# An attention product in which one of sixteen squares is cut in two

## The chip, the cores and the metric

The kernel runs on one core of one Trainium2 chip. The metric is the device time of one execution in microseconds (us); lower is better. A run is executed several times, and the median is compared. TensorE multiplies (the profile calls its matmuls PE and the loading of their weights PEld), VectorE is DVE, ScalarE is ACT, GpSimd is POOL, and SyncE (SP) issues transfers.

## The reference

The reference is a cross-attention with two contexts, all in float32. There are 2 batches of 2048 tokens with 640 channels, in 20 heads of 32 channels. The context has 154 tokens per batch with 1024 channels: 77 of text and 77 of image, each with its own weights for keys and values. Softmax is taken over the 77 text tokens and the 77 image tokens apart, and the two results are added.

```python
residual = hidden_states                       # (2, 2048, 640)
text = encoder_hidden_states[:, :77, :]
ip = encoder_hidden_states[:, 77:, :]
q = _split_heads(hidden_states @ Wq.T, H)      # 20 heads of 32
k = _split_heads(text @ Wk.T, H)
v = _split_heads(text @ Wv.T, H)
out_text = _merge_heads(_attend(q, k, v, sm_scale))
k_ip = _split_heads(ip @ Wk_ip.T, H)
v_ip = _split_heads(ip @ Wv_ip.T, H)
out_ip = _merge_heads(_attend(q, k_ip, v_ip, sm_scale))
out = out_text + IP_SCALE * out_ip             # IP_SCALE = 1
out = out @ Wo.T + bo
return out + residual
```

`_attend` is softmax(q k^T / sqrt(32)) v.

## The kernel before, in words

Channels lie on the 128 partitions, so that 640 channels are 5 chunks of 128, and a chunk is 4 heads of 32. A batch and a chunk together are one attention product `q`, from 0 to 9 (`NP` = 10). The 2048 tokens of a batch are two halves of 1024, so that a unit `u` is half of a `q` and there are 20 units. In the text below, the attention products are numbered in words, from the first to the tenth.

For each unit the queries are projected (`queries`, line 194) and scaled by ScalarE (line 204), and then scores are made in three groups of token tiles (`scores`, line 226). ScalarE copies the scores into the tile `pb` (line 238). VectorE takes the maximum of each row (line 251), POOL subtracts it (line 265), ScalarE takes the exponential (line 272), VectorE sums (line 297) and inverts (line 304), POOL multiplies (line 309), and VectorE transposes every 32x32 block of `pb` in place (line 316). The 154 keys of a token are padded to 160, that is five blocks of 32 (`NK` = 5).

`attend` (line 325) then multiplies the probabilities of a whole `q` by the values. TensorE's array of 128x128 is used as sixteen squares of 32x32. Row group `r` (32 partitions of the input) holds one of four groups of tokens, and column group `g` (32 partitions of the output) is a head. In each of the five rounds `k`, one for each block of keys, there are 16 matmuls, one for each square, in the order r = 0..3 and within it g = 0..3. Each takes 32x32 weights from `v4s` and 512 columns from `pb`, and adds into PSUM bank `pa[r]` at the partitions of `g`. Square n of a round is r = n // 4, g = n % 4; so square 0 is r = 0, g = 0, and square 1 is r = 0, g = 1. The sixteen squares hold different weights and work side by side, and the five rounds of one square add into the same place. ScalarE then copies the four banks into the tile `aT` (`take_attention`, lines 348 and 352).

The rest is the projections of keys and values (line 133), and the output projection: products of fewer multiplications than the plain form for batch 0 (`product`, lines 483 and 493; last chunk in line 464) and for batch 1 (`F` words, line 841), with sums taken by VectorE and POOL.

The order of all work is written out by hand: `SCHEDULE` is a list of words, and `emit` runs each in turn, so that every engine gets its instructions in the order of the words. `A.q@h` is the attention product q into half h of the eight PSUM banks; `CA.q` is the copy behind it. Semaphores between the engines follow from the data; instructions of one engine need none among themselves. The values' squares `v4s` are loaded by DMA from SP (`spread_v`) ahead of each product.

Of the kernel before, what the change touches and what calls it, by code (L numbers as in the profile page):

```python
# [15 lines left out]
H, D, TEXT = 20, 32, 77  # L16
# [4 lines left out]
def kernel(  # L21
# [25 lines left out]
    nc = tc.nc  # L47
# [3 lines left out]
    G = P // D  # L51
# [3 lines left out]
    NT = BLK // P  # L55
    SUB = S // BLK
# [4 lines left out]
    NK = (2 * L + D - 1) // D  # L61
# [3 lines left out]
    NU = NP * SUB  # L65
    OPEN = 4
    HT = TB // 2

    const = ctx.enter_context(tc.tile_pool(name="const", bufs=1))
    qpool = ctx.enter_context(tc.tile_pool(name="qpool", bufs=5))  # L70
# [11 lines left out]
    v4s = [const.tile([P, G, NK, D], F32, name=f"v4_{n}") for n in range(2)]  # L82
# [235 lines left out]
    def attend(q, pa):  # L318

        zones = pb[:, ds(q % 2, SUB)].rearrange("p z n g (k s) -> p (z n) g k s", k=NK)  # L320
        for k in range(NK):
            for r in range(G):
                rows = slice(r * D, (r + 1) * D)
                for g in range(G):
                    nc.tensor.matmul(  # L325
                        pa[r][g * D : (g + 1) * D, :],
                        v4s[q % 2][rows, g, k, :],
                        zones[rows, :, g, k, :],
                        start=(k == 0),
                        stop=(k == NK - 1),  # L330
                    )

    def rows_of_attention(b, c):


        if b == 0:
            return aT[:, ts(c + 1, NHB)]
        if c == 0:
            return aT[:, ts(0, NHB)]
        return aT[:, NHB + c - 1 : NHB + NHB * NHB : NHB]  # L340
# [55 lines left out]
    def block(b, i, r, h):  # L396
# [3 lines left out]
        )  # L400
        return aT[:, m : n + 1 : n - m, ts(h, HT)]

# [38 lines left out]
    def in_dram(t, b, i, s, h):  # L441
        return t[: (NC - 1) * P].rearrange("(op s p) t -> s p op t", s=2, p=P)[
            s, :, :, ds(b * S + i * TB + h * HT, HT)
        ]
# [31 lines left out]
    def product(m, b, i, ps):  # L476
# [3 lines left out]
        for op in range(2):  # L480
            part = ps[:, ts(op, HT)]
            for kp in range(2):
# [8 lines left out]
            if fifth:  # L491
# [3 lines left out]
                    w_last[:, op] if s is None else wo[:, NC - 1, ts(2 * op + s, P)],  # L495
                    rows_of_attention(b, NC - 1)[:, i, ts(h, HT)],
                    start=False,
# [4 lines left out]
    def take_product(m, b, i, ps):  # L502
        part = {2: (0, 0), 1: (0, 0), 5: (1, 1), 7: (1, 1), 3: (0, 1), 6: (0, 1), 4: (1, 0)}[m]
        t = part_in(sums_of(b, i), *part)
        if m in (5, 3, 4, 1 if b else 2):
            for op in range(2):
                bias = bo_sb[:, ds(2 * op + part[0], 1)]
                nc.vector.scalar_tensor_tensor(
                    t[:, op], ps[:, ts(op, HT)], bias, t[:, op], ALU.add, ALU.add
                )  # L510
# [117 lines left out]
    def emit(word):  # L628
# [7 lines left out]
        elif k == "A":  # L636
            at[name] = halves[int(where)]
            attend(x, at[name])
        elif k == "CA":
            take_attention(x, at[f"A.{x}"])  # L640
# [243 lines left out]
```

## Time and profile before

| what | us |
|---|---|
| median of three runs | 500.54 |
| lowest and highest of the three | 499.85, 500.70 |
| the profiled execution | 499.79 |
| its span, first to last instruction | 498.0 |

| engine | busy us | instructions |
|---|---|---|
| TensorE matmul (PE) | 491.1 | 4114 |
| TensorE weight load (PEld) | 291.1 | 4114 |
| VectorE (DVE) | 425.7 | 388 |
| POOL | 425.7 | 189 |
| ScalarE (ACT) | 243.0 | 423 |

| matmuls of | records | busy us |
|---|---|---|
| queries, line 194 | 400 | 178.2 |
| scores, line 226 | 1280 | 57.0 |
| attention products, line 325 | 1600 | 55.7 |
| keys and values, line 133 | 320 | 45.9 |

How to read it: times count from the first instruction. Matmuls overlap in the array, and the end of each is modelled, so that their busy time is no sum of work; the start of each is what the text goes by. In a row of the timeline, instructions of one line are merged: the first number is the start, the second the length until the last of them ends, and x is the count. A row for a narrow window holds the instructions that run in that window, from the start of the first of them. In a row of windows, the stretch is followed by its length and the busy time, with the count of instructions that run in it; then come the granted clock of TensorE, the busy share of the DMA engines and GB/s. The granted clock was full (1.00) throughout. The chain of waits is followed back from the last instruction, and gives the share of the span in which each engine or line held the end.

### The profile page before, as it was taken

The numbers are of one execution on the slowest core, as the hardware profiler recorded it, in microseconds if no ns is written. First come the engines' busy times: TensorE is split into PE (matmuls) and PEld (weight loads), VectorE is DVE, ScalarE is ACT, GpSimd is POOL, SyncE is SP. The second block draws the span as 40 slices with busy tenths as digits, with TensorE's granted clock in tenths as the row PEclk, the third lists the DMA queues.
The fourth block names the chain that finished last, engine by engine and source line by source line (L and its number), as shares of the span: only waits on it lengthen the run. The fifth ranks groups of instructions, "written<-read, shape, count | busy, mean of one in ns | idle before, by whom it ended". The sixth has DMA issues, their size and how long they took to land.

```text
span 498.0 us, 9768 instructions
## 1 busy us (share of the span) xinstructions
PE 491.1 (99%) x4114; PEld 291.1 (58%) x4114; DVE 425.7 (85%) x388; ACT 243.0 (49%) x423; POOL 425.7 (85%) x189
## 2 busy tenths in 40 slices
PE   9999999999999999999999999999999999999997
PEld 4667658558658555457655655744665575444442
DVE  0078998999989899969996888899699999998985
ACT  1276747667757567566616554647473543100000
POOL 0089799999999999998998999899999999397790
PEclk9999999999999999999999999999999999999999
DMA  8985300354253665794074367554524101510026
GB/s 262 355 238 151 108 15 1 86 110 118 57 161 122 177 214 165 247 333 150 1 253 154 123 200 256 151 165 161 200 64 133 45 2 64 169 64 22 0 105 232
DMA packets 66987, 70.15 MB, mean 141 GB/s; under 512 B 3712, under 2 KB 46720, under 8 KB 66944
## 3 DMA queue, kind: packets, MB, share of 16 engines
q1 hardware_dynamic: 66224, 68.81, 44.4%
q8 instruction: 32, 0.52, 0.4%
q10 hardware_dynamic: 720, 0.72, 0.4%
q14 instruction: 11, 0.09, 0.1%
HBM read 58.21 MB, written 11.30 MB: 140 GB/s over the span
## 4 chain that ended last, share of the span: by engine, by line
PE 66%; POOL 15%; DVE 11%; DMA 3%; ACT 2%; issue 2%; SPq 1%; POOLq 0%
PE bank L194 23%; PE bank L841 11%; POOL pb L265 8%; PE bank L325 8%; PE bank L226 8%; PE bank L133 6%; POOL pb L309 6%; PE bank L483 5%; DVE pb L316 4%; PE bank L464 3%; DVE den L297 3%; DVE mx L251 2%; DMA aT<-in_L_xattn_Wk_ip_dram 2%; DMA wq<-in_L_xattn_Wq_dram 2%; PE bank L493 1%
## 5 line engine op out<-in xcount | busy, mean ns | idle before, releaser
L265 POOL TENSOR_TENSOR pb<-pb,mx 128x1848 f32<-128x1848 f32 (+1 forms) x60 | 175.6, 2944 | 32.1 <-DVE mx L251 31.5
L309 POOL TENSOR_TENSOR pb<-pb,rden 128x1848 f32<-128x1848 f32 (+1 forms) x60 | 175.7, 2945 | 13.2 <-DVE rden L304 12.6
L194 PE MATMUL bank<-x,wq 128*128 128x512 f32 x400 | 178.2, 597 | 0.2
L251 DVE TENSOR_REDUCE mx<-pb 128x24 f32<-128x1848 f32 (+1 forms) x60 | 109.8, 1839 | 30.0 <-ACT pb L238 29.6
L272 ACT ACTIVATE pb<-pb 128x1848 f32<-128x1848 f32 (+1 forms) x60 | 94.3, 1578 | 65.6 <-POOL pb L265 65.5
L194 PEld LDWEIGHTS bank<-x,wq 128*128 128x128 f32 x400 | 74.0, 190 | 88.9 <-issue 81.4
L316 DVE STREAM_TRANSPOSE pb<-pb 128x1920 f32<-128x1920 f32 (+1 forms) x60 | 115.4, 1933 | 7.0 <-POOL pb L309 7.0
L297 DVE TENSOR_REDUCE den<-pb 128x24 f32<-128x1848 f32 (+1 forms) x60 | 110.0, 1840 | 11.6 <-ACT pb L272 11.3
L238 ACT COPY pb<-bank 128x462 f32<-128x462 f32 (+1 forms) x240 | 101.9, 536 | 36.7 <-PE bank L226 36.0
L226 PEld LDWEIGHTS bank<-kT,qT 32*128 32x128 f32 x1280 | 46.5, 184 | 23.8 <-issue 16.4
L226 PE MATMUL bank<-kT,qT 32*128 32x154 f32 x1280 | 57.0, 305 | 0.3 <-ACT kT L550 0.3
L325 PE MATMUL bank<-pb,v 32*32 32x512 f32 x1600 | 55.7, 597 | 0.4 <-DVE pb L316 0.3
L133 PE MATMUL bank<-wo_ct,aT 128*128 128x154 f32 x320 | 45.9, 297 | 0.9 <-ACT aT L352 0.4
L204 ACT ACTIVATE qT<-bank 128x512 f32<-128x512 f32 x40 | 23.6, 596 | 46.5 <-PE bank L194 46.5
L133 PEld LDWEIGHTS bank<-wo_ct,aT 128*128 128x128 f32 x320 | 42.9, 188 | 4.4 <-issue 2.4
L325 PEld LDWEIGHTS bank<-pb,v 32*32 32x32 f32 x1600 | 32.1, 103 | 20.8 <-issue 9.5
L464 PE MATMUL bank<-aT,wo_ct 128*128 128x512 f32 x80 | 36.1, 596 | 0.0
L483 PE MATMUL bank<-aT,wo_ct 128*128 128x256 f32 x128 | 32.6, 387 | 0.1
L483 PEld LDWEIGHTS bank<-aT,wo_ct 128*128 128x128 f32 x128 | 23.5, 190 | 7.3 <-issue 3.6
L789 DVE TENSOR_TENSOR x<-x,bank 128x512 f32<-128x512 f32 x36 | 23.1, 681 | 3.4 <-PE bank L841 3.1
L464 PEld LDWEIGHTS bank<-aT,wo_ct 128*128 128x128 f32 x80 | 15.0, 190 | 16.9 <-issue 16.6
L841 PE MATMUL bank<-pb 128*128 128x512 f32 x48 | 22.1, 594 | 0.0
(71 smaller groups left out, 335.1 us busy)
## 6 DMA issues: line engine op xcount, KB each, us to landing
x<-in_x_dram SPq DMA_DIRECT2D x20, 1280.0 KB, 6.8
out_dram<-acc SPq DMA_DIRECT2D x20, 256.0 KB, 2.4
x<-in_x_dram SPq DMA_DIRECT2D x18, 256.0 KB, 5.4
acc<-in_x_dram SPq DMA_DIRECT2D x16, 256.0 KB, 4.1
out_dram<-x SPq DMA_DIRECT2D x15, 256.0 KB, 2.1
v<-scr SPq DMA_DIRECT2D x40, 80.0 KB, 3.3
wq<-in_L_xattn_Wq_dram SPq DMA_DIRECT2D x9, 320.0 KB, 4.9
aT<-in_L_xattn_Wk_dram SPq DMA_DIRECT2D x5, 512.0 KB, 5.4
```

The costliest lines, as they stand in the source:

```text
L133: nc.tensor.matmul(keys_in(out), loaded[n][:, k, :], cT[:, k, :, t, :], start=(k == 0), stop=(k == NCC - 1))
L194: nc.tensor.matmul(pq, wqs[q % 3][:, k, :], xs[place_of(u, h)][:, k, :], start=(k == 0), stop=(k == NC - 1),)
L226: nc.tensor.matmul(ps[g][:, ts(t, 2 * L)], qTs[(u, h)][g * D : (g + 1) * D, ts(st, P)], kT[g * D : (g + 1) * D, c, b].rearrange("p t l -> ...
L238: nc.scalar.copy(keys_of(u, s)[:, :, g], ps[g][:, : n * 2 * L].rearrange("p (n l) -> p n l", n=n))
L251: nc.vector.tensor_reduce(mx, rows_of(u, s), AX.X, ALU.max, negate=by_rows(u, s))
L265: nc.gpsimd.tensor_tensor(rows_of(u, s), rows_of(u, s), maxs[(u, s)].unsqueeze(3).to_broadcast([P, n, 2, L]), ALU.subtract)
L272: nc.scalar.activation(e, e, AF.Exp)
L297: nc.vector.tensor_reduce(dens[(u, s)], rows_of(u, s), AX.X, ALU.add)
L309: nc.gpsimd.tensor_tensor(rows_of(u, s), rows_of(u, s), rdens[(u, s)].unsqueeze(3).to_broadcast([P, n, 2, L]), ALU.mult)
L316: nc.vector.transpose(p, p)
L325: nc.tensor.matmul(pa[r][g * D : (g + 1) * D, :], v4s[q % 2][rows, g, k, :], zones[rows, :, g, k, :], start=(k == 0), stop=(k == NK - 1),)
L483: nc.tensor.matmul(part, w_of[m][:, kp, op], t_of(m, b, i)[:, kp], start=(op == kp == 0 and m in (1, 2, 5)), stop=(op == 1 and kp == 1 and ...
```

## The change

In the first four rounds of each attention product, square 1 is multiplied in two matmuls with the same weights: token tiles 0 to 12 of its 16 (13 x 32 = 416 columns) in its old place, and tiles 13 to 15 (96 columns) behind square 15 of the same round. The fifth round is as before. In the first round the long part opens its place in PSUM (`start`), and the short part adds to it.

```diff
+    LEAD, LONG = 1, 13
...
+        whole, long, short = slice(0, SUB * NT), slice(0, LONG), slice(LONG, SUB * NT)
         for k in range(NK):
-            for r in range(G):
+            steps = [(n, long if n == LEAD and k < NK - 1 else whole) for n in range(G * G)]
+            if k < NK - 1:
+                steps.append((LEAD, short))
+            for n, part in steps:
+                r, g = divmod(n, G)
                 rows = slice(r * D, (r + 1) * D)
-                for g in range(G):
-                    nc.tensor.matmul(
-                        pa[r][g * D : (g + 1) * D, :],
-                        v4s[q % 2][rows, g, k, :],
-                        zones[rows, :, g, k, :],
-                        start=(k == 0),
-                        stop=(k == NK - 1),
-                    )
+                nc.tensor.matmul(
+                    pa[r][g * D : (g + 1) * D, part.start * D : part.stop * D],
+                    v4s[q % 2][rows, g, k, :],
+                    zones[rows, part, g, k, :],
+                    start=(k == 0 and part is not short),
+                    stop=(k == NK - 1),
+                    skip_group_check=(n == LEAD),
+                )
```

## The prediction

> **What bounds the kernel now.** I read the page first, then the records of line 325, then the loads of single products in order of time, then the chain of waits.
>
> ```profile
> span 498.0 us, 9768 instructions
> PE 491.1 (99%) x4114; PEld 291.1 (58%) x4114; DVE 425.7 (85%) x388; ACT 243.0 (49%) x423; POOL 425.7 (85%) x189
> PE 66%; POOL 15%; DVE 11%; DMA 3%; ACT 2%; issue 2%; SPq 1%; POOLq 0%
> PE bank L194 23%; PE bank L841 11%; POOL pb L265 8%; PE bank L325 8%; PE bank L226 8%; PE bank L133 6%; POOL pb L309 6%; PE bank L483 5%; DVE pb L316 4%; PE bank L464 3%; DVE den L297 3%; DVE mx L251 2%; DMA aT<-in_L_xattn_Wk_ip_dram 2%; DMA wq<-in_L_xattn_Wq_dram 2%; PE bank L493 1%
> L464 PE MATMUL bank<-aT,wo_ct 128*128 128x512 f32 x80 | 36.1, 596 | 0.0
> L483 PE MATMUL bank<-aT,wo_ct 128*128 128x256 f32 x128 | 32.6, 387 | 0.1
> L325 PEld LDWEIGHTS bank<-pb,v x1600: 101/103/106, 69.2 to 432.5; 32*32 32x32 f32 x178
> L325 PE MATMUL bank<-pb,v x1600: 584/588/612, 69.2 to 432.9; 32*32 32x512 f32 x178
> ```
>
> TensorE is busy nearly throughout and holds 66% of the chain, but the chain goes through POOL and VectorE for 26%, and there a longer product costs nothing. Line 325 has 8%. Ten attention products of 5 rounds of 16 squares are 800 products; 1600 loads and 1600 matmuls mean that each product is two passes, each a load and a matmul. A round is thus 16 x 4 = 64 TensorE instructions.
>
> Next, the ten products whole: length, and records in each.
>
> ```profile
> 69.20 5.64 PE L325 MATMUL bank<-pb,v 32*32 32x512 f32 x160
> 106.52 5.52 PE L325 MATMUL bank<-pb,v 32*32 32x512 f32 x160
> 143.67 5.64 PE L325 MATMUL bank<-pb,v 32*32 32x512 f32 x160
> 180.92 5.51 PE L325 MATMUL bank<-pb,v 32*32 32x512 f32 x160
> 212.11 5.51 PE L325 MATMUL bank<-pb,v 32*32 32x512 f32 x160
> 261.28 5.57 PE L325 MATMUL bank<-pb,v 32*32 32x512 f32 x160
> 303.71 5.67 PE L325 MATMUL bank<-pb,v 32*32 32x512 f32 x160
> 346.85 5.53 PE L325 MATMUL bank<-pb,v 32*32 32x512 f32 x160
> 392.07 5.55 PE L325 MATMUL bank<-pb,v 32*32 32x512 f32 x160
> 427.96 5.52 PE L325 MATMUL bank<-pb,v 32*32 32x512 f32 x160 [0.25 <-DVE pb L316]
> ```
>
> Inside the fourth (from 180.92), the weight loads in order of time; the last two of these rows are from narrower windows of the same view. Then two instants of the seventh.
>
> ```profile
> 180.89 0.27 PEld L325 LDWEIGHTS bank<-pb,v 32*32 32x32 f32 x32 [0.16 <-issue]
> 181.35 0.10 PEld L325 LDWEIGHTS bank<-pb,v 32*32 32x32 f32 x1 [0.19 <-issue]
> 181.78 0.57 PEld L325 LDWEIGHTS bank<-pb,v 32*32 32x32 f32 x32 [0.33 <-issue]
> 181.97 0.10 PEld L325 LDWEIGHTS bank<-pb,v 32*32 32x32 f32 x1
> 185.19 0.33 PEld L325 LDWEIGHTS bank<-pb,v 32*32 32x32 f32 x24
> ...
> 181.35 1.35 PE L325 MATMUL bank<-pb,v 32*32 32x512 f32 x24
> ...
> 304.30 1.14 PE L325 MATMUL bank<-pb,v 32*32 32x512 f32 x17
> 304.92 0.18 PEld L325 LDWEIGHTS bank<-pb,v 32*32 32x32 f32 x7
> ```
>
> All 32 loads of round 1 go within 0.27 us. At 181.35 square 0 starts its second pass, 0.43 after its first (180.92), and the 33rd load (square 0, round 2) goes at once; the 34th waits for the matmul that it follows (181.78, another 0.43). Then the 35th, square 1's, waits until 181.97. That is 0.62 after square 0's second pass of round 1 began (181.35): its 0.588 record and 0.03. In the seventh product the second pass of square 4 began at 304.30 (the first still running at 304.80, squares 0 to 3 being out by then) and the round-2 load of square 5 went at 304.92, again 0.62 later. So I read: TensorE holds 64 instructions, one round, in order; a place is free only when the instruction 64 before has ended, with all ahead of it. A square of round k+1 may load 0.62 after the square **before** it began its second pass of round k. From a square's first load to its second pass is 0.46 (180.89 to 181.35), so a round takes 0.62 + 0.46 = 1.08, where two passes of 0.43 are 0.86. In each round the wave's end comes forward by one square's place, as each square follows its left neighbour. The 24 loads of 12 squares from 185.19 take 0.33 - 0.10 = 0.23, about 18 ns a square.
>
> **The change part by part.** Nothing moves on a DMA queue, SP, POOL, VectorE or ScalarE. Per product 4 squares become two: 4 x 2 more loads and as many matmuls, 160 of each in all; no columns are added.
>
> *The two sizes.* No row has 96 or 416 columns. From the L464 and L483 rows, (596 - 387) / 256 = 0.82 ns a column: estimates of 0.08 and 0.34 us of streaming, as ends 0.02 and 0.43 (another slope; a whole pass). In round 1, counted from its start, square 1's long passes run 0.03 to 0.37 and 0.37 to 0.72, and the first short pass 0.72 to 0.80. This fits, as the other squares run until about 1.0.
>
> *The places in the queue.* Instructions 65 to 68 are now the short piece, not square 0 of round 2. The 67th entry is free at once; the 68th, the short second pass, needs instruction 4, square 0's second pass, out: 0.43 + 0.62 = 1.05. So the short piece ends at about 1.15 and square 0 of round 2 loads at 1.05, not 0.43. It loses its lead, which nobody used: before, square 1 waited until 181.97 - 180.92 = 1.05 anyway. Square 1 starts at 1.15, late by 0.1; it is one of 16 starting over 1.05 to 1.31, so I cost it at zero; without the cover of the other squares it costs 0.1 us.
>
> *The lockstep.* With 68 instructions a round, a square hangs on **its own** second pass of the round before, no longer on its left neighbour's. The period stays 1.08, but the wave no longer gains a place each round. From round 2 to round 5 that loses 3 places of 18 ns, 54, and I take 0.06 us per product. Ends: 0, if the neighbour rule is kept after all, and 0.05 + 0.10 = 0.15, if square 1's late start of 0.1 is not covered in the end.
>
> *Products that stagger in round 1.* In some, semaphore waits split round 1 by groups of four squares.
>
> ```profile
> L325 PEldq EVENT_SEMAPHORE  x2: 51/51/51, 261.3 to 261.5; - x2
> 303.70:303.75 0.05, 0.04 (x4) 1.00 1.05 410
> 303.87:303.90 0.03, 0.03 (x8) 1.00 0.88 341
> 304.01:304.04 0.03, 0.03 (x12) 1.00 1.57 614
> 304.14:304.15 0.01, 0.01 (x14) 1.00 1.57 614
> ```
>
> In the seventh product 4, 8, 12 and then more matmuls are under way at 303.70, .87, 304.01, .14: steps of about 0.14. The first, second, third, sixth and seventh product have such a wait ahead of the last four squares (the sixth's two waits, the later at 261.5, are shown). Now the last square of round 5 hangs, three places back, on a square ahead of that gap; after the change on itself, behind it. I take 0.12 us for each, as the gap is partly worked off by the 18 ns pitch; ends 0.06 (the gap is worked off wholly) and 0.06 + 0.14 = 0.20.
>
> *What reaches the end.* The chain in order of time: its pieces around the products that it leaves out, and one product that it goes through.
>
> ```profile
> 137.47 8.28 POOL pb L265 x3
> ...
> 179.04 3.29 POOL pb L265
> ...
> 212.11 5.51 PE bank L325 x153
> ...
> 391.78 2.22 POOL pb L265
> ```
>
> It passes by the products at 143.67, 180.92 and 392.07, where POOL and VectorE hold it: 0.12 + 0.06 + 0.06 is hidden, and counts if that cover is gone. The other seven it goes through as it does at 212.11: three unstaggered (212.11, 346.85, 427.96) and four staggered ones, 3 x 0.06 + 4 x 0.12 = **0.66 us**. All ten would give 5 x 0.06 + 5 x 0.12 = 0.90. The ends: 0 and 5 x 0.15 + 5 x 0.20 = 1.75. The profiled execution took 499.79, 0.75 below the median of the three runs (500.54); 499.79 + 0.66 = 500.45, and from the median **501.2**.
>
> *A rule of the skill against the change.* At 181.35 a load goes into rows on which squares 0 to 3 are still multiplying (second passes of 0.588 from 181.35 on). The Trainium skill, "TensorE: Matmul & The Clock Gate", Part 3, "What overlaps and what doesn't", says that a weight load overlaps matmuls under way only where their row group is another one. By that rule the short piece would be far dearer (last rival below); the trace does not agree, since the load of 181.35 did not wait. The same page gives the queue as 64 deep with a partial reorder window; by that figure the sum stays 0.66, and the first and second rivals below lose, since both need a wait that is no queue.
>
> **The rivals.**
> 1. *Faster.* The wait of 0.19 (181.78 to 181.97) is no queue: it falls only on a tile that goes on without a break, as square 0 does. The short piece then breaks square 0's run. Square 2 of round 2 would load at 0.94 instead of 1.08 (0.72 + 0.19 for the second short load, then two loads), and later rounds would take 0.34 + 0.34 + 0.03 + 0.19 + 0.02 = 0.92 instead of 1.08: 0.14 + 3 x 0.16 = 0.62, less 0.05 for the lost lead, 0.57 on seven products: 4.0 us, 496.5. Against it: only square 0 got its load of round 2 ahead (the 33rd) and ran on; square 4 in the row of 304.30 did not, and still square 5 waited 0.62 for it.
> 2. *No change.* Each square's own results must drain, and the queue is wide enough. Then the neighbour rule stays as it was, and the extra pieces cost two loads: about 0.02 per product, 0.1 in all: 500.6. The rows of before cannot tell this from the queue, since a round is just 64 instructions; but 32 loads and one more and then nothing is what 64 places look like.
> 3. *Slower.* A short piece holds its four places as long as a whole square, 1.08. Then a round costs 68/64 of 1.08, 0.067 more; over four rounds 0.27, on seven products 1.9, on ten 2.7: 502.4 to 503.2. It decides once the piece's places are wanted before it has ended. By my working it ends about 0.4 us before the last square of the next round needs them, which is a thin margin with the short second pass entering so late.
> 4. *Slower by far.* Loads wait for the whole row group: each short pass then waits until squares 2 and 3 are out (1.06), and costs its own 0.08, a drain of 0.16 (0.588 - 0.43) and 0.03, twice; the next round starts at 1.62 instead of 1.05. 0.57 x 4 rounds x 7 to 10 products: 517 to 523.
>
> **How the numbers follow.** A change of 0.2%, 1.0 us, is about what a measurement of this kernel tells from none, as its three runs spread over 0.85. The lost lead: 0.50, its own range 500.5 to 502.3 (0 to 1.75 on the median), of which 0.32 within 0.2% and 0.18 slower. Rival 1, with partial gains of the same kind: 0.19, faster. Rival 2: 0.10, same. Rival 3: 0.19, slower. Rival 4: 0.02, slower. Faster 0.19, same 0.42, slower 0.39. The range 498.2 to 503.2 takes in part of rival 1's gain and all of rival 3; outside are rival 4, the full gain of rival 1 and a loss above 2.7.
>
> **What would show it.** Right: 1680 records of loads and matmuls on the product's line, 176 in each product; lengths of about 5.57 for the unstaggered ones (the ones at 181 and 212) and 5.64 to 5.80 for the staggered; in the first round no load of square 0 at +0.43, but one of the short piece at about +0.38 and square 0's at +1.05; round after round 1.08 apart. Rival 1 shows as rounds of 0.92 and products of about 5.0; rival 3 as rounds of 1.14; rival 4 as products near 7.8. The ends on the chain: the product at 212 should pass its 0.06 on, the one at 181 should not. My forecast is wrong if the products get shorter at all, if the short piece's second pass starts well before +1.05 (then places are not freed in order), or if the chain goes through other products afterwards.

## The result, and the profile after

The changed kernel takes 504.16 us (median of five executions, 502.86 to 505.40) where the kernel before takes 500.54 (499.85 to 500.70). The ratio is 1.008, with a 95% interval of 1.0057 to 1.0103: slower by 0.8%, and above the predicted range of 498.2 to 503.2. The profiled execution of the changed kernel took 502.86, and its span is 501.1; the kernel before had 499.79 and 498.0. The traces explain these 3.07 us. The median lies 1.3 above the profiled execution, and the times scatter three times as widely as before; only the profiled execution has a trace, so that the cause of the scatter can only be inferred.

First the page of the changed kernel: span, busy time, chain by engine, the two groups of the product's line (330 now), and the queue that brings instructions.

```profile
span 501.1 us, 9928 instructions
PE 493.7 (99%) x4194; PEld 289.2 (58%) x4194; DVE 425.9 (85%) x388; ACT 242.9 (48%) x423; POOL 425.6 (85%) x189
PE 80%; POOL 8%; DVE 8%; issue 2%; ACT 1%; POOLq 0%
L330 PE MATMUL bank<-pb,v 32*32 32x512 f32 (+2 forms) x1680 | 58.1, 577 | 1.1 <-issue 0.9
L330 PEld LDWEIGHTS bank<-pb,v 32*32 32x32 f32 x1680 | 29.4, 103 | 26.6 <-issue 23.2
q8 instruction: 33, 0.54, 0.4%
```

And the rows of the page before that answer to the last three.

```profile
L325 PE MATMUL bank<-pb,v 32*32 32x512 f32 x1600 | 55.7, 597 | 0.4 <-DVE pb L316 0.3
L325 PEld LDWEIGHTS bank<-pb,v 32*32 32x32 f32 x1600 | 32.1, 103 | 20.8 <-issue 9.5
q8 instruction: 32, 0.52, 0.4%
```

There are 80 matmuls and 80 loads more, as in the prediction's 1680 records of each. (Its "160 of each in all" is a slip: 160 is the number of both together.) New are 0.9 us of idle time ahead of matmuls that no engine ended ("issue"), and one more packet on the queue for instructions: 33 packets, 0.54 MB, so 16 KB each.

The ten products of the changed kernel, as the prediction showed them: start, length to the last end, records (168 matmuls each).

```profile
68.92 5.80 PE L330 MATMUL bank<-pb,v 32*32 32x512 f32 x168
106.38 5.64 PE L330 MATMUL bank<-pb,v 32*32 32x512 f32 x168
143.69 5.93 PE L330 MATMUL bank<-pb,v 32*32 32x512 f32 x168
181.21 5.89 PE L330 MATMUL bank<-pb,v 32*32 32x512 f32 x168
212.72 5.52 PE L330 MATMUL bank<-pb,v 32*32 32x512 f32 x162
219.13 1.05 PE L330 MATMUL bank<-pb,v 32*32 32x512 f32 x6 [0.89 <-issue]
263.85 5.68 PE L330 MATMUL bank<-pb,v 32*32 32x512 f32 x168
306.40 5.79 PE L330 MATMUL bank<-pb,v 32*32 32x512 f32 x168
349.67 5.59 PE L330 MATMUL bank<-pb,v 32*32 32x512 f32 x168
394.95 5.61 PE L330 MATMUL bank<-pb,v 32*32 32x512 f32 x168
430.81 5.59 PE L330 MATMUL bank<-pb,v 32*32 32x512 f32 x168
```

The fifth product stands in two rows: after 162 of its 168 matmuls nothing starts until 219.13, and it lasts 7.46 us (212.72 to 220.18) instead of 5.51. Set against the rows of before, product by product, from the records' own nanoseconds:

| product | 1st | 2nd | 3rd | 4th | 5th | 6th | 7th | 8th | 9th | 10th | sum |
|---|---|---|---|---|---|---|---|---|---|---|---|
| longer by, us | 0.16 | 0.12 | 0.29 | 0.37 | 1.95 | 0.11 | 0.12 | 0.06 | 0.07 | 0.06 | 3.32 |
| forecast, us | 0.12 | 0.12 | 0.12 | 0.06 | 0.06 | 0.12 | 0.12 | 0.06 | 0.06 | 0.06 | 0.90 |

The eleven stretches between and around the products give -0.26 together, -0.28 of it ahead of the first product. 3.32 - 0.26 is the 3.07 of the profiled executions. So the whole loss lies in the products, and nearly all of it reaches the end. Seven of them are as forecast within 0.04; the third, fourth and fifth are 0.17, 0.31 and 1.89 above, 2.37 in sum.

Round 1 of the fourth product looks as the prediction drew it. Its weight loads in order of time:

```profile
181.21 0.23 PEld L330 LDWEIGHTS bank<-pb,v 32*32 32x32 f32 x32 [0.16 <-issue]
181.59 0.10 PEld L330 LDWEIGHTS bank<-pb,v 32*32 32x32 f32 x1 [0.15 <-issue]
181.94 0.10 PEld L330 LDWEIGHTS bank<-pb,v 32*32 32x32 f32 x1 [0.24 <-issue]
182.28 0.53 PEld L330 LDWEIGHTS bank<-pb,v 32*32 32x32 f32 x33 [0.24 <-issue]
```

The short piece loads 0.38 after the start and again 0.73 after it; square 0 of round 2 comes at 1.07, no longer at 0.43. The short piece's second matmul starts at 1.07 too, where the prediction had 1.05. What goes wrong in the fifth product is of another kind. The end of it, from the timeline of all engines in a narrow window:

```profile
216.43 1.81 PE L330 MATMUL bank<-pb,v 32*32 32x512 f32 x40
216.99 0.34 PEld L330 LDWEIGHTS bank<-pb,v 32*32 32x32 f32 x26 [0.19 <-issue]
...
219.13 0.15 PEld L330 LDWEIGHTS bank<-pb,v 32*32 32x32 f32 x6 [1.80 <-issue]
219.13 1.05 PE L330 MATMUL bank<-pb,v 32*32 32x512 f32 x6 [0.89 <-issue]
```

The last start ahead of the gap is at 217.65, the next at 219.13, and by 218.24 the array has run empty. No semaphore and no engine ends that wait. The queue of 64 does not either, since its places are all free by then. The stretches around it, with the DMA engines' share and rate as the last two columns:

```profile
212.50:215.50 3.00, 2.98 (x104) 1.58 (x101) 3.00 (x3) 1.89 (x4) 2.56 (x3) 1.00 1.09 356
215.50:217.70 2.20, 2.20 (x91) 1.04 (x61) 2.20 (x2) 0.00 (x0) 2.20 (x1) 1.00 1.15 238
217.70:219.10 1.40, 0.54 (x20) 0.00 (x0) 0.20 (x1) 0.95 (x2) 1.40 (x2) 1.00 1.05 319
```

The share of the DMA engines (the time of all packets, so that it can pass 1) stays above 1.0 through all three stretches. And in the transfers between 216.3 and 217.8 there is one packet for instructions, which by its record moved from 216.34 to 217.72:

```profile
q1 hardware_dynamic: 355, 0.32, 108.8%
q8 instruction: 1, 0.02, 5.8%
```

This gave the theory for the experiments, called the supply theory below: TensorE's instructions come in blocks of 16 KB over the same DMA engines as the data. An attention product uses them up fast, 64 in 1.07 us for five rounds on end, while a projection of queries takes 0.43 us for a load and a matmul; a group of scores is nearly as dense, but is over after 24 to 40 matmuls and their loads. Where a limit between two blocks falls into a product and the next block is late, TensorE stands still. The change adds 160 instructions, and so moves every later limit to another place in the work.

### The profile page after: what moved, and what is told of

It reads as the page before. It is cut to its first block, busy times and chain, and to the rows that moved or that the text cites. A ratio compares the mean times of both kernels' runs of the same rounds, so it can differ in the third digit from the quotient of the medians.

```text
span 501.1 us, 9928 instructions
## 1 busy us (share of the span) xinstructions
PE 493.7 (99%) x4194; PEld 289.2 (58%) x4194; DVE 425.9 (85%) x388; ACT 242.9 (48%) x423; POOL 425.6 (85%) x189
## 4 chain that ended last, share of the span: by engine, by line
PE 80%; POOL 8%; DVE 8%; issue 2%; ACT 1%; POOLq 0%
PE bank L195 31%; PE bank L847 11%; PE bank L330 10%; PE bank L227 9%; PE bank L134 9%; PE bank L489 5%; POOL pb L310 4%; POOL pb L266 4%; PE bank L470 3%; DVE pb L317 3%; DVE den L298 2%; DVE mx L252 1%; PE bank L499 1%; POOL aT L430 1%; PE bank L546 1%
## 5 line engine op out<-in xcount | busy, mean ns | idle before, releaser
L330 PE MATMUL bank<-pb,v 32*32 32x512 f32 (+2 forms) x1680 | 58.1, 577 | 1.1 <-issue 0.9
L330 PEld LDWEIGHTS bank<-pb,v 32*32 32x32 f32 x1680 | 29.4, 103 | 26.6 <-issue 23.2
L358 ACT COPY aT<-bank 128x256 f32<-128x256 f32 x40 | 11.5, 413 | 23.3 <-PE bank L330 23.3
```

Of the source, the lines that this page charges most:

```text
L330: nc.tensor.matmul(pa[r][g * D : (g + 1) * D, part.start * D : part.stop * D], v4s[q % 2][rows, g, k, :], zones[rows, part, g, k, :], star ...
```

## The experiments

Times and ratios are against the kernel before on the same chip (medians of 499.99 to 500.12); the ratios are those on record, which differ from the quotient of the medians by up to 0.2%. "Longer by" is the sum over the ten products in the profiled execution, against the profile of before.

**e1: the change, its instructions moved by 132.** Seven warm-up matmuls ahead of all work become forty small ones, so that each product starts 132 entries later in TensorE's order (a matmul here is two passes with a load each).

```diff
-    for _ in range(7):
-        nc.tensor.matmul(banks[0][:, :P], warm, warm, start=True, stop=True)
+    for _ in range(40):
+        nc.tensor.matmul(banks[0][:D, :D], warm[:, :D], warm[:, :D], start=True, stop=True)
```

> The cut as in the change; the 7 warm-up matmuls (128 columns) are replaced by 40 small ones (32 columns), so that TensorE's later instructions stand 132 places further on. Theory (instruction supply): TensorE's instructions come 256 at a time, and a product stalls when two limits between such blocks fall into it. With 132 places only the ninth product has two. So the stalls in the third, fourth and fifth product (0.17, 0.31 and 1.89 us) go, every product has the length of the lost lead alone (5.57 to 5.80 us), and the time is 500.9 to 501.6. Rival (the cut itself holds the queue): the fifth product stays near 7.5 us and the time near 503 to 504.

Measured: 502.29 us, ratio 1.004 (1.0028 to 1.0052). The third, fourth and fifth product:

```profile
144.98 5.75 PE L330 MATMUL bank<-pb,v 32*32 32x512 f32 x168
182.32 5.58 PE L330 MATMUL bank<-pb,v 32*32 32x512 f32 x168
213.82 5.57 PE L330 MATMUL bank<-pb,v 32*32 32x512 f32 x168
```

All three stalls are gone with the program's real work untouched; the fifth product is 0.05 longer than before. The ten are longer by 1.09, the rest of the span by 1.15. Of this 0.79 lies ahead of the first product; there the small warm-ups take longer, and the first projection starts at 5.11 instead of 4.42. The time is 0.7 above the 500.9 to 501.6 that were expected: the stalls went as the theory had it, and the dearer start was not in the sum. The first two products are 0.23 and 0.21 longer, a little more than in the change; why was not found.

**e2 and e3: the kernel before, moved by 132 and by 100.** The same edit in the kernel before, which has no cut square; e3 with 32 small matmuls for 40.

> The kernel before with the same 132 places: what the small matmuls cost at the start, expected 0 to 0.5 us. Theory (instruction supply): the fifth product gets a limit at its very first instructions and the next 256 later, at the start of its fifth round, so a stall of 0 to 1.2 us there, although nothing is cut; all others as before. Rival (the cut itself): all products within 0.03 us of before.

> The kernel before with 100 places (32 small matmuls instead of the 7). Theory (instruction supply): the first, second and fifth product now have two limits; the fifth, whose transfers are the busiest, stalls by about 1 us, the first and second by 0 to 0.3. Rival (the cut itself): all products within 0.03 us of before and the time at most 0.5 us above it.

Measured: e2 504.19 us, ratio 1.0085 (1.0063 to 1.0107); e3 505.23, 1.0083 (1.0057 to 1.0109). The fifth product of e2:

```profile
213.97 4.45 PE L325 MATMUL bank<-pb,v 32*32 32x512 f32 x128
220.73 1.15 PE L325 MATMUL bank<-pb,v 32*32 32x512 f32 x32 [2.31 <-issue]
```

A kernel without the change stalls as the changed one does: its product stops dead after 128 matmuls, with 2.89 us from one start to the next, and the other nine are within 0.02 of before. The stall of 2.40 is twice the largest that was expected. Part of e2's loss is the start again (1.91): the small warm-ups, and behind them waits for the first loads of `x`, which come in some executions without any edit there (e7). In e3 the fifth product is 3.41 longer and something follows it, which the last section shows. So the cut is not needed for the stall; its place in the order is.

Counting gives the place. The load or matmul behind the gap has the same number in TensorE's stream of records in every kernel that stalls there, whatever it belongs to:

| behind a gap | kernels | records ahead of it |
|---|---|---|
| in the fifth product | the change, e2, e3, e7 | 4244 |
| in the sixth product | e5, e7, e8, e9 | 5001 |
| in the eighth product | e5, e8 | 6524 |

Between the first and the second lie 757 records and 11 semaphore instructions, which the records leave out: 768, three times 256. Between the second and the third lie 1523 and 13: 1536, six times 256. A block of 16 KB with 256 instructions has 64 bytes for each. The Trainium skill, "Runtime: NRT & Kernel Launch", "Instruction fetch mechanics", says that engines are refilled in such blocks of 256 by DMA while the current block runs, and that crossing a limit is mostly hidden. The runs agree with the size of the block; hidden it is not here, at 1.89 us in the changed kernel and 2.4 in e2.

With the limits so found, the changed kernel has two of them within one product in the third (instructions 48 and 304 of 336), the fourth (10 and 266), the fifth (69 and 325) and the tenth (27 and 283), and stalls in the first three of these. Set beside e1's products, the first weight load that comes late is the next one at or behind the second limit in each: by 0.32 us in the third, 0.30 in the fourth and 1.91 in the fifth. The kernel before has two limits in its fourth and ninth product and one in its fifth, at instruction 133 of 320, and no gap of such a size at any. Between two limits in a product lie 256 instructions, or four rounds, 4.3 us.

The packets show what a stall is made of. In the changed kernel the fifth product crosses its first limit at 213.76, the packet begins to move only at 216.34, 2.57 later, and work goes on 1.41 after the packet has ended. Over the 14 runs no block was begun earlier than 1.25 us after the end of its packet, and behind all gaps of the table it was begun 1.26 to 1.71 after it. So where two limits lie 4.3 us apart, it is the wait of the packet before it moves that decides whether the second one costs nothing or stalls.

**e4: eight squares less.** The kernel before without squares 8 to 15 in rounds 2 to 5, to measure the queue of the prediction by itself. With 32 instructions a round, a square hangs on one two rounds back if 64 places set the pace; if every square has to drain for itself, it hangs on its own.

```diff
-            for r in range(G):
+            for r in range(G if k == 0 else 2):
...
-                        stop=(k == NK - 1),
+                        stop=(k == (NK - 1 if r < 2 else 0)),
```

> Leaves out squares 8 to 15 in the last four rounds of each product: a round is 32 TensorE instructions there. Theory (a queue of 64 in order): two rounds fit in the queue, a square no longer waits for its neighbour's drain, and rounds come 0.86 us apart; the last matmul of an unstaggered product starts 4.20 us after the first, where before it is 4.93. Rival (each square must drain before it goes on): rounds stay 1.08 apart and the last start is at 4.8 to 4.9.

Measured: one execution, 496.9 us; two of the products without a wait in them:

```profile
180.88 4.78 PE L325 MATMUL bank<-pb,v 32*32 32x512 f32 x96
345.14 4.79 PE L325 MATMUL bank<-pb,v 32*32 32x512 f32 x96
```

The last start comes 4.19 to 4.27 us after the first (4.78 less the last record's 0.59), where 64 places give 4.20 and a drain of each square's own 4.8 to 4.9. The queue theory of the prediction holds.

**e5 and e6: three warm-ups, with and without the change.** Sixteen instructions fewer ahead of everything (`range(7)` becomes `range(3)`).

> The cut as in the change, with 3 of the 7 warm-up matmuls, so that all of TensorE's later instructions stand 16 places further ahead and the start costs nothing. Theory (instruction supply): the limit in the fifth product now falls behind its end, so its 1.89 us go; the third has its second limit near its end and may keep 0.2 to 0.6 us, the fourth, sixth and tenth come out within 0.3. The time is 500.8 to 501.6, 0.8 to 1.4 us over the uncut kernel with 3 warm-up matmuls: the lost lead (0.7 to 0.95) and a little. Rival (the cut itself holds the queue): still about 504.

> The kernel before with 3 of the 7 warm-up matmuls: the control of the run above. Theory (instruction supply): only the ninth product holds two limits, as it does before, so no stall over 0.05 us anywhere, and the time is that of before within 0.5 us. Rival (fewer warm-up matmuls leave TensorE slow at the start): 1 us or more above before.

Measured: e5 506.96 us, ratio 1.0142 (1.0118 to 1.0166); e6 501.49, 1.0024 (1.0015 to 1.0034). The fifth product of e5 is clean as expected (0.06 longer), and yet e5 is far slower than the 500.8 to 501.6 that were expected. Its sixth and eighth product:

```profile
264.65 4.58 PE L330 MATMUL bank<-pb,v 32*32 32x512 f32 x130
269.60 2.12 PE L330 MATMUL bank<-pb,v 32*32 32x512 f32 x38 [0.37 <-issue]
352.67 4.36 PE L330 MATMUL bank<-pb,v 32*32 32x512 f32 x116
358.83 3.62 PE L330 MATMUL bank<-pb,v 32*32 32x512 f32 x52 [1.80 <-issue]
```

The stall of the fifth is exchanged for others: the third product is 0.41 longer, the sixth 1.50, the seventh 0.93 and the eighth 4.26, where the granted clock was also halved for 3.4 us behind the gap. Ahead of the stall in the eighth, three transfers of 1280 KB had been issued since 347.5, and the block came only at 356.44, 8.5 us after the limit before it. I had counted places and not looked at which transfers stood in the way. e6 has the same 16 instructions fewer and its products are 0.02 longer in sum, with no stall, as expected; its time is 1.4 above before and not within 0.5, and in the profiled execution the loss is a slow start (0.89).

**e8: the same cut in two halves.** As e5, with 256 columns in place and 256 behind (`LONG` = 8).

> As the run with 3 warm-up matmuls, but the cut is 256 and 256 columns instead of 416 and 96. Theory (the lost lead comes from four more instructions in a round, whatever their size): every product is within 0.05 us of that run, and the time within 0.4 us. Rival (the short piece costs by its size): 0.1 us and more per product, 1 us and more in all.

Measured: 508.75 us, ratio 1.0173 (1.0157 to 1.0189). The second, fourth, fifth and ninth product, which have no stall in either kernel, are the same to the nanosecond (first to last start 5058, 5001, 4981 and 5027 in both). How the square is divided does not matter to them; the number of instructions does. The time is 1.8 above e5 and not within 0.4 as expected: both have stalls at the same instructions, and the times scatter so much (e5 alone runs from 505.75 to 510.07) that the 1.8 says nothing of the cut.

**e7 and e9: fewer transfers beside the fifth product.** In the changed kernel the two loads of `x` that are issued from 214.33 on go some 18 us later (e7); in e9 also the loads of partial sums and of the residual, issued from 206.56 on, go some 60 us earlier (145.14). In the list of words, `LX` and `LF` are those loads.

```diff
-        "LX.14.0 cm5.0 m2.0@7 cm2.0 cm1.0 M2.12 LX.13.1 G6.0 N2.10 D1.11 R0.12@0 m3.0 K0.12 S2.11 I1.11 E0.11 "
-        "R1.12@0 K1.12 D0.11 m6.0 st.0.4 M0.12 G7.0 q.14.0@2 E2.11 cm3.0 LX.13.0 q.13.1@1 D2.11 I2.11 N0.10 "
+        "cm5.0 m2.0@7 cm2.0 cm1.0 M2.12 G6.0 N2.10 D1.11 R0.12@0 m3.0 K0.12 S2.11 I1.11 E0.11 "
+        "R1.12@0 K1.12 D0.11 m6.0 st.0.4 LX.14.0 LX.13.1 M0.12 G7.0 q.14.0@2 E2.11 cm3.0 LX.13.0 q.13.1@1 D2.11 I2.11 N0.10 "
```

and for e9 besides

```diff
-        "K2.7 M0.7 S0.7 T1.6 M2.7 LX.10.0 R1.7@0 K1.7 k.4.0@4 ck.4.0 SQ.3 M1.7 E0.7 LK.19 D0.7 I0.7 S2.7 E2.7 "
+        "K2.7 M0.7 S0.7 T1.6 M2.7 LF LX.10.0 R1.7@0 K1.7 k.4.0@4 ck.4.0 SQ.3 M1.7 E0.7 LK.19 D0.7 I0.7 S2.7 E2.7 "
...
-        "E0.10 E1.10 D2.10 D0.10 D1.10 q.12.1@1 cq.12.1 R1.11@1 LF I1.10 o.0@3 co.0 N1.10 K1.11 M1.11 S1.11 "
+        "E0.10 E1.10 D2.10 D0.10 D1.10 q.12.1@1 cq.12.1 R1.11@1 I1.10 o.0@3 co.0 N1.10 K1.11 M1.11 S1.11 "
```

> The change, with the two loads of x (1280 KB each) that go out at 214.33, in the fifth product, put behind the next store of results, which goes out at about 231. Nothing of TensorE's stream moves, so the limits stay where they are in the changed kernel. Theory (instruction supply, late because its blocks wait behind these transfers): the stall in the fifth product falls from 1.89 us to 0.6 or less. Rival (the supply is as slow without them): it stays at 1.5 to 2.2.

> The change with all large loads taken out of the stretch of the fifth product: the two loads of x behind the store at about 231, as in the run before, and the five loads of the residual (acc and res, 1.3 MB), which go out at 206 to 210, moved ahead to about 150. TensorE's stream is that of the change, so the limits between its blocks stay. The run with the two late loads alone had the engines still full of these others until 217.5, when the block of instructions came. Theory (a block of instructions waits behind data transfers): in the fifth product the block now comes about 1 us earlier or more and the stall falls from 1.89 us to 0.6 or less. Rival (a block takes as long on quiet engines): the stall stays at 1.5 to 2.2.

Measured: e7 505.88 us in its one execution, with the fifth product 1.97 longer, as without the edit, against what was expected: the engines were still full with the earlier loads until about 218, and the packet moved 2.6 us after the first limit as before, so the two of `x` were not what the block waited for. Its sixth product is 2.02 longer, with a stall that the change did not have. e9 503.47, ratio 1.0047 (1.0030 to 1.0065). The fifth and sixth product of e9:

```profile
213.74 5.57 PE L330 MATMUL bank<-pb,v 32*32 32x512 f32 x168
262.96 4.46 PE L330 MATMUL bank<-pb,v 32*32 32x512 f32 x122
268.14 2.19 PE L330 MATMUL bank<-pb,v 32*32 32x512 f32 x46 [0.71 <-issue]
```

and the stretches of the fifth:

```profile
213.00:215.00 2.00, 1.98 (x71) 1.19 (x74) 2.00 (x2) 1.62 (x4) 2.00 (x2) 1.00 0.78 156
215.00:217.00 2.00, 2.00 (x72) 1.05 (x62) 2.00 (x3) 0.62 (x2) 1.56 (x2) 1.00 0.00 0
217.00:219.00 2.00, 2.00 (x77) 0.92 (x66) 1.92 (x1) 0.00 (x0) 2.00 (x2) 1.00 0.00 0
```

With the DMA engines quiet from 215 on, the product crosses the very same two limits and takes 5.57, 0.06 over before. Its packet begins to move at 214.86, 0.07 after the first limit and not 2.57. In the fifth product the block is therefore late because of the other transfers, and the cause of the 1.89 is shown from both sides: move the limit (e1) or clear the DMA engines (e9). The moved loads of the residual then stand beside the third product, which is 0.91 longer. The 1.79 of the sixth is not explained by them: they had landed long before, and its packet moved only at 265.58, 3.92 after the limit before it, though the DMA engines had been idle from 262 to 263. What else makes a packet wait is open.

**e10 and e11: the stagger taken away in the kernel before.** The prediction took the waits in round 1 for the arrival of the four row groups' values. In e10 one transfer brings them all.

```diff
-        for r in range(G):
-            nc.sync.dma_start(
-                out=v4s[q % 2][r * D : (r + 1) * D].rearrange("p g k d -> p g (k d)"),
-                in_=scr[q].rearrange("(g d) l -> d g l", g=G),
-            )
+        nc.sync.dma_start(
+            out=v4s[q % 2].rearrange("p g k d -> p g (k d)"),
+            in_=scr[q].unsqueeze(0).to_broadcast([G, D, G * LP]),
+        )
```

e11 is e10 with the second product's transfer (`VS.1`) two steps earlier, ahead of the word `LK.11`.

> The kernel before, uncut, with the values of a product brought by one DMA instead of four, from a scratch laid out for it, so that the first round of a product waits for one transfer and not for four. Theory (a stagger in round 1 is carried to the end of the product by the queue): all ten products last about 5.51 to 5.55 us, 0.4 to 0.6 us less in all, and the time is 0.3 to 0.7 us below before if no limit between blocks falls badly. Rival (the stagger is hidden by the other squares): products as before, no change.

> The kernel before, uncut, with the value squares spread by one transfer in place of four, and the spread of the second step issued ahead of the first key loads that it stood behind. If what staggers the first rounds is the arrival of the four row groups' values, all ten products stay at 5.51 to 5.55 us (0.47 less than before in sum), and the second product now starts as early as in the kernel before (within 0.2 us), where with the single transfer alone it started 1.01 late. The time is then 499.8 to 500.2, 0.3 to 0.7 below the kernel before. The rival: the products' staggers were hidden all along, and the time stays within 0.2 of the kernel before.

Measured: e10 500.46 us, ratio 1.0003 (0.9994 to 1.0012); e11 499.90, 0.9997 (0.9989 to 1.0006). The first two products of e10, then of e11:

```profile
69.25 5.52 PE L324 MATMUL bank<-pb,v 32*32 32x512 f32 x160
107.45 5.51 PE L324 MATMUL bank<-pb,v 32*32 32x512 f32 x160 [0.94 <-DMA v<-scr]
```

```profile
69.50 5.52 PE L324 MATMUL bank<-pb,v 32*32 32x512 f32 x160
107.19 5.51 PE L324 MATMUL bank<-pb,v 32*32 32x512 f32 x160 [0.44 <-DVE mx L250]
```

All ten products last 5.51 to 5.55 in both, 0.47 less in sum, as expected: the stagger is the values' arrival. (The second product, which had 5.52, had next to none to lose.) The gain is given back ahead of the second product, which starts 1.01 later than before in e10 and still 0.51 later, counted from the end of the first, in e11. The expectation of e11 missed there: by its row the product waits for VectorE now, but in the kernel before it started 0.44 ahead of the end of that same instruction, so that it is more likely still the transfer, and this was not settled. Neither version beats the kernel before by more than the measurement can tell, so the expected 0.3 to 0.7 us did not show.

**e12: the short piece in another place.** As e1, with the 96 columns directly behind the 416.

```diff
-                steps.append((LEAD, short))
+                steps.insert(LEAD + 1, (LEAD, short))
```

> The kernel of run e1 (the change, with 132 more queue places in front), with the 96 columns directly behind the 416 instead of at the end of the round. Queue theory (64 places in order): the short piece takes its places in the middle of the round, so the last squares of the round enter late and begin their first pass behind the drain; the last start in a product comes about 0.14 us later than in e1, the unstaggered products take 0.2 instead of 0.06 more than before, and the sum over ten rises by about 1.4 us, 503 to 504. The rival (only the number of columns and loads counts, the place in the queue does not): product lengths as in e1 within 0.03 and the time within 0.5 of it.

Measured: 502.34 us, ratio 1.0041 (1.0025 to 1.0056). The fourth and the tenth product:

```profile
182.32 5.73 PE L330 MATMUL bank<-pb,v 32*32 32x512 f32 x168
430.45 5.73 PE L330 MATMUL bank<-pb,v 32*32 32x512 f32 x168
```

5.73 where e1 has 5.58 and 5.59: the 0.14 of the queue theory, eight products being 0.16 to 0.24 longer than before. Of the staggered ones only the third and sixth took something on top, and the first got shorter, so that the sum is 1.86 and not about 2.5 (e1: 1.09). The time, however, is within 0.1 of e1, where 503 to 504 was expected: 0.34 of the 0.77 came back between the products in the profiled pair (0.81 there against 1.15), and the rest is within the scatter of four and five executions. Products went by the queue, the time by the rival.

## Why the prediction was wrong

**The two sizes, the places in the queue, the lockstep: right.** The record of a pass of 96 columns is 0.24, and less the drain of 0.16 that is the 0.08 of the working. The loads of round 1 came at 0.38 and 1.07 as drawn (0.38 and 1.05). The chain of the changed kernel has the rounds of the fifth product 1.07 apart. The eighth, ninth and tenth product are 0.06 to 0.07 longer, which is the lost lead of three places. e4 and e12 confirm the queue in kernels that the reading was not taken from.

**Products that stagger in round 1: right in size.** 0.16, 0.12, 0.11 and 0.12 for the first, second, sixth and seventh, where 0.12 was said; and e10 shows that what staggers them is the values' arrival. That the last square hangs behind the gap, as the prediction had it, was not tested by itself: no run has the cut without the stagger.

**What reaches the end: wrong, and for a reason that the profile of before held.** The third, fourth and ninth product were left out since the chain passes them by. But behind the third and fourth the stretches are only 0.03 and 0.05 shorter in the changed kernel, and its chain goes through both products, from 143.71 and from 181.28 on, which was the prediction's own sign of being wrong. Its piece for the third:

```profile
143.71 5.92 PE bank L330 x72
```

Behind the ninth the stretch is 0.09 shorter, so that its 0.07 may have been hidden as forecast. The chain names one of several paths of nearly equal length. TensorE's idle time is the better witness: in the kernel before the gaps ahead of its matmuls sum to 3.4 us, 1.05 of them ahead of the first one. An engine with so few gaps has little room to hide a longer step. In size this step is at most 0.24, the difference between 0.66 and 0.90.

**What no step had: the supply of the added instructions.** This is the step that failed. "Nothing moves on a DMA queue", said where the change is taken part by part, was false: 160 more instructions of 64 bytes are 10 KB more, and every limit between blocks behind them moves. The added loads and matmuls were costed as places in the queue, and their fetching at nothing, without a name for what hides it. It is 2.37 of the 3.32 us (0.17, 0.31 and 1.89 in the third, fourth and fifth product). It is likely most of the scatter too, as e1, without the stalls, runs from 501.89 to 502.41 only; but the slower executions have no trace to show it. It is this term that the prediction lacked; with the 0.90 of all ten products it makes the 3.3 measured. The profile of before held the hints: 32 packets of instructions, a DMA share of 1.57 inside a product, and products that use 256 instructions in 4.3 us. The size of a stall could not be read from it, as that kernel has none.

**The rivals.** No product became shorter, which ends the first. The second falls with the 0.06 on every product and with e4. The third is out although its 502.4 to 503.2 lie closest to the time: its rounds of 1.14 are nowhere, and in e1, where the cut and its queue are as in the change, the products lose 1.09 and not 2.7. The fourth needed products near 7.8; the one product near that length has its loss in one gap at a limit, not in its rounds.

That the median came within 1 us of the third rival is chance. What the cut costs without the stalls is 1.09 in e1's products, about 0.2% of the time. e1 measures 0.4% with its dearer start. What the stalls cost is a matter of luck in the placement: the same shift repairs the changed kernel and spoils the one before.

## What to carry to other kernels

Instructions are fetched over the same DMA engines as the data: where many short ones run close together beside heavy transfers, count them in blocks, find the limits, and see that a block's fetch has quiet DMA engines. Any added or removed instruction moves all later limits, so a small edit can lose or win microseconds far from its place, and a comparison of two versions should look for "issue" gaps at limits before it blames the edit. And where an engine has hardly any gaps, expect a longer step on it to count, even where the chain of waits passes by.

## What the runs showed of the hardware

- Blocks of 256 instructions, 16 KB in one packet of 0.9 to 2.0 us. With quiet DMA engines a product crosses two limits at no cost (e9, a share of 0.02 between them). With a share of 0.7 to 1.1 from one limit to the next, the gaps of the table were 0.95 to 2.9 us from start to start. The share alone does not decide it: the tenth product of the changed kernel had 0.78 between its limits and no gap. A block is begun 1.25 us after its packet's end at the earliest; what that time is was not found.
- A stall can be followed by a slower clock. In e3, whose fifth product started nothing from 217.00 to 219.24, the granted clock (third column from the end) fell to half from 219.41 to 226.23:

```profile
219.20:221.00 1.80, 1.76 (x16) 0.18 (x16) 0.00 (x0) 0.00 (x0) 1.80 (x2) 0.56 1.05 388
221.00:224.00 3.00, 3.00 (x12) 1.39 (x5) 0.65 (x1) 2.88 (x4) 3.00 (x2) 0.50 1.00 364
224.00:227.00 3.00, 3.00 (x5) 1.18 (x5) 2.80 (x3) 2.59 (x2) 0.80 (x2) 0.63 0.05 16
```

  Matmuls of 512 columns then started 0.85 us apart instead of 0.43 for some 5 us, and 2.55 us were lost behind the product. The Trainium skill, "TensorE: Matmul & The Clock Gate", Part 1, gives the idle time after which the clock is halved as about 3.4 us; here a gap of 2.24 between starts was enough, while the 2.89 of e2 in the same place left the clock at 1.00. What decides it is open.
- A packed product of sixteen 32x32 squares is bound here by the 64 places and not by the array: rounds of 1.07 for 0.86 of streaming, and with eight squares in a round (e4) rounds of the 0.86.
